# A one-core transformer block: a planner that counts SyncE's issues and the queues' transfers, and a re-cut order of its steps

## The chip, the cores and the metric

The kernel runs on one core of one Trainium2 chip. The metric is device time in microseconds (us), the median of several runs; lower is better. Where one profiled execution is read, its own time and its span are given beside the median. Engines are named as in the profile: PE (TensorE matmul), PEld (its weight loads), DVE (VectorE), ACT (ScalarE), POOL (GpSimd), SP (SyncE, which issues nearly all DMAs from one in-order queue).

## The reference

One transformer block with conditioning, in float32. Eight sequences of 1024 tokens, width 512, 16 heads, hidden width 2048:

```python
mod = silu(condition) @ Wada + bada
sh_a, sc_a, gt_a, sh_m, sc_m, gt_m = split(mod, 6, axis=1)
xm = layernorm(x, g1, be1) * (1 + sc_a) + sh_a
x = x + gt_a * attention(xm, Wqkv, Wproj, bproj)      # causal, softmax
xm = layernorm(x, g2, be2) * (1 + sc_m) + sh_m
x = x + gt_m * (gelu(xm @ W1 + b1) @ W2 + b2)
```

## The kernel before, in words

**Blocks and steps.** The tokens are cut into 16 blocks of 512 (`NB` is 16): block n is the first half (n even) or the second half (n odd) of a sequence; the keys of a second half are twice as many, so odd blocks have more attention. For each block there are dense steps, which the code calls linear: `at` (make the normalized, modulated, transposed input of attention), `k`, `q`, `v`, `proj`, `mt` (the same input for the feed-forward part), `u` 0 to 3 (up) and `d` 0 to 3 (down). `k`, `q`, `v` and `u` are done by seven products of half-size blocks instead of eight (`strassen`), with sums of the weights made once and kept in device memory. All matmuls of one product go through one of three PSUM banks (`lin_bank`).

**Attention.** A group is one block and four heads. Scores units (`scores`, tiles `sc`) only find row maxima, on DVE; weights units (`weights_T`, tiles `st`) compute the scores again, transposed, with the maximum subtracted, and ACT takes the exponential into `pT`. Both use the one PSUM tile `st`, so each unit waits until DVE or ACT has read the one before. POOL masks the diagonal of `pT` (`affine_select`) and adds the units of a group up; `weigh` multiplies by v (tile `po`); `finish` sums over keys, and DVE inverts.

**Who decides the order.** The order of all engines' instructions is decided while the program is built. `plan[w]` lists the dense steps beside the attention of block w; window 16 (`plan[NB]`) holds the rest. A small planner keeps a clock per engine (`now`), notes each instruction with a fixed cost (`note`, `note_pe`, `note_act`), and remembers when each value is written (`written`) and each buffer is left (`left`). Dense steps are generators which yield what they need; `step_aside` and `work` put dense matmuls between attention units until the next unit's needs are met by the planner's clock. `run_jobs`, `run_act_jobs` and `run_pool_jobs` let small DVE, ACT and POOL jobs into those engines' queues when the planner believes them free.

**DMAs before.** Weights come through a ring of eight 256 KB buffers (`RING`, `fetch`, `release`); a weight's load stands in SP's queue as soon as the buffer eight places back is used up, and waits there. The planner of the kernel before has no clock for SP or for the DMA queues: a weight counts as there at once, and other transfers get fixed times: `LANDING` 10000 ns for gate rows, residual tiles and moved k and v, `HOLDING` 8000 ns for each half of a turn. A turn (`turn`) transposes 12 to 14 of the blocks' inputs through device memory: DVE transposes small blocks, one DMA writes them out (`held`), four DMAs read them back in another order (`hat`), ACT or DVE scale them into `xm`.

**Other names the change touches.** `combine_out` (line 193) adds a PSUM bank to something in SBUF on DVE. `either` (lines 158 and 161) puts an addition on DVE or POOL, by the planner's clocks. `bias_row` (line 522) loads one gate row into the single buffer `rowgb`, which the row before it must have left; `project_out` issues it for the feed-forward part at its end, `load_xr` for attention. `scores_by_heads` (lines 1518 to 1535) does a scores unit in two of the banks, when the planner sees no dense work for 3000 ns. `beside` in the plan starts a step as a thread beside the main one.

Of the kernel before, what the change touches and what calls it, by code (L numbers as in the profile page):

```python
# [22 lines left out]
def kernel(  # L23
# [70 lines left out]
    now = {"PE": 0.0, "DVE": 0.0, "ACT": 0.0, "POOL": 0.0}  # L94
# [5 lines left out]
    COLUMN = 0.84  # L100
    table = [None]
# [10 lines left out]
    def note(engine, ns, reads=(), writes=(), port=False):  # L112
        start = max(now[engine], due(reads, writes))
        if port:
            start = max([start] + [b for a, b in pool_spans if a <= start < b])
        end = start + ns
        now[engine] = end
        if engine == "POOL":
            pool_spans.append((start, end))
            del pool_spans[:-16]  # L120
        for k in reads:
            left[k] = max(left.get(k, 0.0), end + SYNC)
        for k in writes:
            written[k] = end + SYNC
        return end

# [112 lines left out]
    for w in range(1, NB):  # L239
# [7 lines left out]
        if w == NB - 1:  # L247
            steps = late[:1] + rows_a + [("proj", n), ("mt", n)] + late[1:]
            steps += rows_m + own + m[3:5] + [("load_xr", w)] + m[5:6]
            late = m[6:]  # L250
        else:
# [9 lines left out]
            steps += [("q", w + 1)] + early_v + rows_m + own  # L261
# [10 lines left out]
    plan[NB] = [late[0], ("beside", late[1]), ("proj", n), ("mt", n)] + mlp_steps(n)  # L272
# [56 lines left out]
    ring, used, taken = [], set(), [0]  # L329

    def fetch():

        while len(ring) < len(order) and (len(ring) < RING or len(ring) - RING in used):
# [24 lines left out]
    def release(*indices):  # L358
        used.update(indices)
        fetch()  # L360
# [23 lines left out]
    def load_x(n):  # L384
# [3 lines left out]
        for t in range(NTT):  # L388
            some = x[b, h * TB + t * P : h * TB + (t + 1) * P, :]
            if f"a{n}" in by_pe:  # L390
                nc.sync.dma_start(rows[:, t, :], some)
            else:
                nc.sync.dma_start(rows[ts(t, Q), :, :], some.rearrange("(t i) d -> i t d", i=Q))
        return rows
# [39 lines left out]
    def modulation(i):  # L434
# [5 lines left out]
        yield [], [BANK]  # L440
        bank = lin_bank()
        pm = banks[bank][:, : NC * B].rearrange("p (c b) -> p c b", b=B)
        for c in range(NC):
            for k in range(NC):
                w = part[k // 2, c // 2][:, k % 2, ts(c % 2, P)]
                matmul(pm[:, c, :], w, condT[:, k, :], k == 0, k == NC - 1, bank=bank)
# [32 lines left out]
    def gates(kind):  # L479
# [11 lines left out]
        yield [], [BANK]  # L491
# [14 lines left out]
        note("DVE", 700, port=True)  # L506
        for name, row in ((f"g{kind}", b_gate), (f"gb{kind}", b_out)):
            kept_rows[name] = kept.tile([B, D], F32, tag=f"kept_{name}", name=f"kept_{name}")
            nc.sync.dma_start(kept_rows[name], row)

    def gate_broadcasts(b, kind):
# [4 lines left out]
        gate_rows[name] = row  # L516

    def bias_row(n, kind):
# [5 lines left out]
        written["row", f"gb{kind}", n] = now["PE"] + LANDING  # L524
# [143 lines left out]
    def turn(key, rows, xm):  # L668
# [17 lines left out]
        written["held", key] = now["PE"] + HOLDING  # L686
# [4 lines left out]
        written["turned", key] = now["PE"] + HOLDING  # L691
# [76 lines left out]
    def accumulate(pairs, reads=(), close=True):  # L768
        yield reads, [BANK]
        bank = lin_bank()  # L770
        for i, (lhsT, rhs) in enumerate(pairs):
            if i:
                yield [], []
            matmul(banks[bank], lhsT, rhs, i == 0, close and i == len(pairs) - 1, reads, bank)
# [11 lines left out]
    def keep(w, i, a, piece):  # L786
        at = kept.tile([P, D], F32, tag=f"kept_{LABEL[id(w)]}_{i}_{a}", name=f"kept_{LABEL[id(w)]}_{i}_{a}")
        kept_sums[id(w), i, a] = at
        nc.sync.dma_start(at, piece)

    def weight_sums(step, part):
# [4 lines left out]
        for j, (out, a, b, op) in enumerate(SUMS):  # L796
# [4 lines left out]
            keep(w, i, out, stage[:, j, :])  # L801
# [5 lines left out]
    def preparation():  # L807
# [5 lines left out]
        def load(w, i):  # L813
# [6 lines left out]
            loaded.append((w, i, got, now["PE"] + 12000))  # L820

        load(*todo.pop(0))
        while loaded:
# [5 lines left out]
            for out, a, b, op, name in IN_PLACE:  # L829
# [3 lines left out]
                keep(w, i, name, got[out])  # L833
# [26 lines left out]
    def strassen(step, x, dest, target, row, done):  # L860
# [14 lines left out]
        def product(a, t, bank=None):  # L875
            start = bank is None
            reads = [(x, t)] + ([("sums", *step, a)] if raw and a[0] == "S" else [])
            for i in range(2):
# [141 lines left out]
    def project_out(n):  # L1020
# [14 lines left out]
        for t, xt in enumerate(tiles):  # L1035
            if last:
# [8 lines left out]
            else:  # L1045
                bank = yield from accumulate(
                    [(attT[:, c, ts(t, P)], piece(at[c])) for c in range(NC)], [("att", n)]
# [18 lines left out]
        bias_row(n, "m")  # L1066
# [3 lines left out]
    def up(step):  # L1070
# [16 lines left out]
        if (n, q) == (0, 0):  # L1087
            yield ["prepared up"], []
        written["g", n, q] = NEVER
# [30 lines left out]
    def store(n, t):  # L1120
        unstored.setdefault(n, 2)

        def when_added():
            yield [("xr", n, 2 * t), ("xr", n, 2 * t + 1)], []
            nc.sync.dma_start(some_rows(out, n, t), residual[n][:, half(t, 2), :])
            unstored[n] -= 1
# [5 lines left out]
    def load_xr(n):  # L1132
# [7 lines left out]
        for t in range(NTT):  # L1140
            written["xr", n, t] = now["PE"] + LANDING
# [3 lines left out]
        row = ("row", "gba", n)  # L1145
        for t in range(NTT):
            job = lambda t=t: add_to(xr[:, t, :], gate_rows["gba"], [row], [("xr", n, t)])
            pool_jobs.append((job, [("xr", n, t), row]))
        written["xr begun", n] = 0.0

    def down(n, part):
# [19 lines left out]
        def product(operand):  # L1171
# [3 lines left out]
            for i in range(NQ):  # L1175
                p = next(at)
                for k in range(2):
# [4 lines left out]
                    for m in range(2):  # L1182
                        if bank is None:
                            yield reads, [BANK]
                            bank = lin_bank()
                        else:
# [5 lines left out]
                            c + m == 0, c == 2 * NQ - 1, reads, bank,  # L1192
# [44 lines left out]
        if part == 0:  # L1237
            yield [("g", n, 0), ("g", n, 1), "prepared", ("row", "gbm", n)], []
            for i in range(NTT):
                add_to(residual[n][:, i, :], gate_rows["gbm"], [("row", "gbm", n)], [("xr", n, i)])  # L1240
            combine(nc.vector, "B12", "B12", "B11")
# [26 lines left out]
        else:  # L1268
# [16 lines left out]
            for q in range(NQ):  # L1285
                hTs.pop((n, q))


    def perform(step):
# [9 lines left out]
        elif kind == "load_xa":  # L1299
            x_pre[step[1]] = load_x(step[1])  # L1300
            written["x", f"a{step[1]}"] = now["PE"] + 6000
# [564 lines left out]
    for n in range(NB):  # L1866
        written["attended", n] = NEVER
        written["v done", n] = NEVER
        written["stored", n] = NEVER
        written["xr begun", n] = NEVER  # L1870
# [75 lines left out]
```

## Time and profile before

| | |
|---|---|
| time, median of 3 runs | 3536.86 us (3535.36 to 3538.43) |
| the profiled execution's own time | 3537.37 us |
| its span, first to last instruction | 3534.7 us |
| mean granted TensorE clock | 0.995 |
| PE busy | 3461.9 us, 98% |
| DVE, POOL, ACT busy | 2201.4, 2054.0, 1208.4 us |

How to read it. Each timeline row is: start in us from the span's start, length in us, engine, line of the kernel, operation, tile written and tiles read, shapes, number of instructions merged into the row, and in brackets the idle time of the engine just before the row with what ended it. Busy PE time includes time at a lowered clock; the rows of stretches give the granted clock (1.00 is full speed) after the busy times of the engines.

### The profile page before, as it was taken

How to read it: one execution, taken by the hardware profiler on the slowest of the kernel's cores; microseconds unless marked ns; L12 is line 12 of the kernel's file. 1: busy time of each engine (PE TensorE's matmuls, PEld its weight loads, DVE VectorE, ACT ScalarE, POOL GpSimd, SP SyncE). 2: the span in 40 equal slices, each digit the busy share in tenths (PEclk: the TensorE clock that was granted, in tenths of full speed). 3: DMA queues.
4: the chain of work that ended last, by engine and by line, in shares of the span. 5: the costliest groups of instructions: out<-in, count | busy, mean ns of one | idle time of the engine just before them, and what ended most of it. 6: DMA issues, size and time to landing. Idle time of an engine off the chain costs nothing. (4 is left out here: it accounts for less than half of the span.)

```text
span 3534.7 us, 120362 instructions
## 1 busy us (share of the span) xinstructions
PE 3461.9 (98%) x54429; PEld 1732.1 (49%) x54429; DVE 2201.4 (62%) x2438; ACT 1208.4 (34%) x1264; POOL 2054.0 (58%) x2228
## 2 busy tenths in 40 slices
PE   8999999999999999999999999999999999999999
PEld 4444445454454545445454444544555445554445
DVE  5776675565657666665566666665666756655463
ACT  2334323352233523335233442333423343223431
POOL 2666846566357663756727566375753658537560
PEclk9999999999999999999999999999999999999999
DMA  6753434435445445353453534545354545443334
GB/s 199 239 167 106 136 115 138 138 112 157 136 127 152 111 155 153 120 160 118 135 155 119 167 112 147 149 138 145 116 158 136 154 130 147 132 134 98 114 91 140
DMA packets 328195, 491.11 MB, mean 139 GB/s; under 512 B 27260, under 2 KB 177596, under 8 KB 324100
## 3 DMA queue, kind: packets, MB, share of 16 engines
q1 hardware_dynamic: 327568, 483.39, 46.1%
q8 instruction: 428, 7.01, 0.8%
q14 instruction: 83, 0.68, 0.1%
q10 hardware_dynamic: 116, 0.03, 0.0%
HBM read 425.57 MB, written 55.64 MB: 136 GB/s over the span
## 5 line engine op out<-in xcount | busy, mean ns | idle before, releaser
L1769 POOL TENSOR_TENSOR pT<-pT,pT 128x256 f32<-128x256 f32 (+3 forms) x1254 | 1214.4, 1003 | 330.0 <-PE po L1679 186.9
L1651 ACT ACTIVATE pT<-st 128x2048 f32<-128x2048 f32 x288 | 541.0, 1878 | 1059.3 <-PE st L1639 952.3
L202 PE MATMUL bank<-w,hT 128*32 128x256 f32 x14336 | 822.7, 380 | 0.5 <-issue 0.5
L1563 DVE TENSOR_REDUCE mx<-sc 128x4 f32<-128x2048 f32 (+3 forms) x381 | 658.9, 1750 | 228.1 <-PE sc L1548 222.3
L202 PEld LDWEIGHTS bank<-w,hT 128*32 128x32 f32 x14336 | 446.5, 110 | 392.7 <-issue 111.6
L202 PE MATMUL bank<-xm_m,w 128*32 128x256 f32 x8192 | 498.5, 382 | 1.6 <-ACT xm_m L750 0.8
L202 PE MATMUL bank<-t_m,w 128*32 128x256 f32 x6144 | 381.6, 380 | 0.6 <-DVE t_m L762 0.6
L1656 POOL TENSOR_SCALAR_AFFINE_SELECT pT<-pT 128x512 f32<-128x512 f32 x256 | 173.6, 696 | 342.3 <-ACT pT L1651 339.8
L202 PEld LDWEIGHTS bank<-xm_m,w 128*32 128x32 f32 x8192 | 256.2, 110 | 223.9 <-issue 56.4
L1560 DVE TENSOR_TENSOR sc<-sc,mask 128x1024 f32<-128x1024 f32 (+1 forms) x158 | 161.5, 1022 | 309.8 <-PE sc L1548 246.5
L1548 PE MATMUL sc<-kT,qT 32*128 32x512 f32 (+3 forms) x3048 | 329.4, 522 | 8.3 <-ACT pT L1651 4.4
L1679 PE MATMUL po<-pT,v 128*32 128x512 f32 (+3 forms) x3048 | 302.0, 491 | 3.8 <-POOL pT L1656 3.6
L1639 PE MATMUL st<-qT,kT 32*128 32x512 f32 (+3 forms) x3072 | 303.8, 488 | 0.0
L202 PEld LDWEIGHTS bank<-t_m,w 128*32 128x32 f32 x6144 | 189.4, 110 | 172.8 <-issue 46.9
L1718 DVE RECIPROCAL rec<-rec 128x128 f32<-128x128 f32 x256 | 227.3, 922 | 49.0 <-ACT rec L1709 49.0
L202 PE MATMUL bank<-xm_a,w 128*32 128x256 f32 x3968 | 241.7, 380 | 0.0
L202 PE MATMUL bank<-w,qT 128*32 128x512 f32 x2048 | 238.4, 599 | 1.1 <-DMA w<-in_L_cond_Wproj_dram 1.1
L1548 PEld LDWEIGHTS sc<-kT,qT 32*128 32x128 f32 x3048 | 130.3, 184 | 191.0 <-issue 94.4
L193 DVE TENSOR_TENSOR hT<-bank,u_u 128x512 f32<-128x512 f32 x192 | 130.4, 687 | 112.0 <-PE bank L202 108.8
L202 PE MATMUL bank<-t_a,w 128*32 128x256 f32 x2944 | 185.3, 381 | 1.4 <-DVE u_d L193 1.4
L1076 ACT ACTIVATE hT<-hT,cols 128x512 f32<-128x512 f32 x256 | 164.6, 711 | 47.8 <-DVE hT L193 47.2
L202 PEld LDWEIGHTS bank<-xm_a,w 128*32 128x32 f32 x3968 | 124.6, 110 | 106.4 <-issue 27.6
(227 smaller groups left out, 3386.3 us busy)
## 6 DMA issues: line engine op xcount, KB each, us to landing
w<-in_L_cond_W_dram SPq DMA_DIRECT2D x384, 256.0 KB
w<-kept_up_S SPq DMA_DIRECT2D x256, 256.0 KB
w<-kept_down_S SPq DMA_DIRECT2D x256, 256.0 KB
w<-kept_qkv_S SPq DMA_DIRECT2D x180, 256.0 KB
w<-in_L_cond_Wqkv_dram SPq DMA_DIRECT2D x147, 256.0 KB
hat_a<-in_x_dram SPq DMA_DIRECT2D x64, 256.0 KB
xr<-in_x_dram SPq DMA_DIRECT2D x32, 512.0 KB
w<-in_L_cond_Wproj_dram SPq DMA_DIRECT2D x64, 256.0 KB
```

Source lines behind the costliest of these rows:

```text
L193: nc.vector.tensor_tensor(out, src, other, op)
L202: nc.tensor.matmul(ps[r, :], columns, rhs, start=start, stop=stop, skip_group_check=True)
L1076: nc.scalar.activation(hT[:, i, :], hT[:, i, :], AF.Gelu, bias=cols[:, O_B1 + f : O_B1 + f + 1])
L1548: nc.tensor.matmul(sc[:, j, c0 : c0 + w], qTs[n][r, gg, ts(qt, P)], keys_of(n, kh)[r, gg, :w], start=True, stop=True, skip_group_check=True,)
L1560: nc.vector.tensor_tensor(place, place, shape_of.to_broadcast(place.shape), ALU.add)
L1563: nc.vector.tensor_reduce(maxima[n, gg][:, kh, qt, :], sc[:, :, c0 : c0 + w], axis=AX.X, op=ALU.max)
L1639: nc.tensor.matmul(st[:, j, c0 : c0 + w], kT[r, gg, ts(k % NTT, P)], qT[r, gg, TB - w :], start=False, stop=True, skip_group_check=True,)
L1651: nc.scalar.activation(pT[:, :, :used], st[:, :, :used], AF.Exp, scale=scale)
L1656: nc.gpsimd.affine_select(diagonal, diagonal, pattern=[[0, HPG], [1, P]], compare_op=ALU.is_ge, fill=0.0, base=0, channel_multiplier=-1,)
L1679: nc.tensor.matmul(po[r, TB - w :], v[:, k % NTT, g * P + j * hd : g * P + (j + 1) * hd], pT[:, j, c0 : c0 + w], start=(k == 0), stop=last ...
L1718: nc.vector.reciprocal(some, some)
L1769: nc.gpsimd.tensor_tensor(into, into, pT[:, j, c0 : c0 + w], ALU.add)
```

## The change

The planner gets clocks for SP and for the DMA queues. `note_dma` adds 425 ns of issue to SP's clock, then lets the transfer begin 1000 ns later or when the queues' clock is free, adds a given length (680 ns for a 256 KB weight, 2600 for `held`, 1250 for each of the four reads back), and takes the data as there 1200 ns after that. It is called at each DMA in place of the fixed times for those (moved k and v keep theirs). Steps now yield the weights that they read, so that the planner lets PE come to a weight only when it believes it landed.

Five things that are not bookkeeping: `combine_out` may copy the bank with ACT and add afterwards, where DVE's clock is 3500 ns behind ACT's; `run_act_jobs` lets jobs into ACT's queue up to 1500 ns ahead of PE's clock; `project_out` starts one waiting POOL job ahead of each tile, and no longer issues the feed-forward gate row at once, but in a thread that waits until the planner believes the row buffer free; the first `u` of the last block waits for the end of `d` of the block before; and the plan is re-cut: `v` stands ahead of `q` in even windows from 4 on, in window 15 `d` 13/2 comes ahead of `proj` 14, and `d` 14/1 moves from window 15 to window 16.

```diff
+    ISSUE, BEGIN, LAND = 425, 1000, 1200
+    def note_dma(ns, reads=(), writes=(), after=0.0):
+        begun = max(now["SP"], due(reads, ()), after)
+        now["SP"] = begun + ISSUE
+        now["DMA"] = max(begun + BEGIN, now["DMA"]) + ns
+        for k in writes:
+            written[k] = now["DMA"] + LAND
...
     def combine_out(out, bank, src, other, reads=(), writes=(), op=ALU.add, last=True):
-        nc.vector.tensor_tensor(out, src, other, op)
-        note("DVE", 690, [("l", bank), *reads], writes)
+        ready = due([("l", bank)], writes)
+        if op is ALU.add and out is not other and max(now["DVE"], ready) > max(now["ACT"], ready) + 3500:
+            nc.scalar.copy(out, src)
+            note_act(585, None, [("l", bank)], writes)
+            either(out, out, other, op, [*reads, *writes], writes)
+        else:
+            nc.vector.tensor_tensor(out, src, other, op)
+            note("DVE", 690, [("l", bank), *reads], writes)
...
         if w == NB - 1:
-            steps = late[:1] + rows_a + [("proj", n), ("mt", n)] + late[1:]
-            steps += rows_m + own + m[3:5] + [("load_xr", w)] + m[5:6]
-            late = m[6:]
+            steps = late[:2] + rows_a + [("proj", n), ("mt", n)] + late[2:]
+            steps += rows_m + own + m[3:5] + [("load_xr", w)]
+            late = m[5:]
...
-            steps += [("q", w + 1)] + early_v + rows_m + own
+            steps += early_v + [("q", w + 1)] + rows_m + own
...
-    plan[NB] = [late[0], ("beside", late[1]), ("proj", n), ("mt", n)] + mlp_steps(n)
+    plan[NB] = late[:-1] + [("beside", late[-1]), ("proj", n), ("mt", n)] + mlp_steps(n)
...
             w = wp.tile([P, D], F32, tag="w", name=f"w_{i}")
+            note_dma(680, [], [("w", i)], freed.get(i - RING, 0.0) + 300)
...
-        yield [], [BANK]
+        yield [("w", i) for i in at], [BANK]
...
-            everything or (min(now["ACT"], now["DVE"]) <= now["PE"] and due(act_jobs[0][1]) <= now["PE"])
+            everything or (min(now["ACT"], now["DVE"]) <= now["PE"] + 1500 and due(act_jobs[0][1]) <= now["PE"])
...
         nc.sync.dma_start(held, small_blocks)
-        written["held", key] = now["PE"] + HOLDING
+        note_dma(2600, [("blocks", key)], [("held", key)])
         yield [("held", key)], []
         for m in range(NTT):
             some = held[:, ts(m, D)].rearrange("(a i) d -> i a d", i=Q)
             nc.sync.dma_start(rows[ts(m, Q), :, :], some)
-        written["turned", key] = now["PE"] + HOLDING
+            note_dma(1250, [("held", key)], [("turned", key)])
...
+            if pool_jobs and not last:
+                pool_jobs.pop(0)[0]()
...
-        bias_row(n, "m")
+        def next_row():
+            yield ["rowgb free"], []
+            bias_row(n, "m")
+        written["row", "gbm", n] = NEVER
+        start(next_row())
...
+        if (n, q) == (NB - 1, 0):
+            yield [("down done", n - 1)], []
```

More of the change, by code (lines that the diff above doesn't have):

```diff
@@ L91 @@
     NB = len(blocks)
-    now = {"PE": 0.0, "DVE": 0.0, "ACT": 0.0, "POOL": 0.0}
+    now = {"PE": 0.0, "DVE": 0.0, "ACT": 0.0, "POOL": 0.0, "SP": 0.0, "DMA": 0.0}
     written, left = {}, {}
@@ L359, in release @@
         used.update(indices)
+        for i in indices:
+            freed.setdefault(i, now["PE"])
         fetch()
@@ L509, in gates @@
             nc.sync.dma_start(kept_rows[name], row)
+            note_dma(200, [("gate", kind)])
     def gate_broadcasts(b, kind):
@@ L523, in bias_row @@
         gate_rows[f"gb{kind}"] = row
-        written["row", f"gb{kind}", n] = now["PE"] + LANDING
+        note_dma(900, ["rowgb free"], [("row", f"gb{kind}", n)])
     jobs = []
@@ L773, in accumulate @@
                 yield [], []
-            matmul(banks[bank], lhsT, rhs, i == 0, close and i == len(pairs) - 1, reads, bank)
+            landed = [("w", i) for i in uses[i : i + 1]]
+            matmul(banks[bank], lhsT, rhs, i == 0, close and i == len(pairs) - 1, [*reads, *landed], bank)
+            if free:
+                freed[uses[i]] = now["PE"]
         return bank
```

48 lines of the change are left out of this document (31 added, 17 removed).

## The prediction

> **What bounds the kernel now.** I read the page's span and shares first, then the timeline of PE for every wait of it, then the stretches with a lowered clock, and then, at the longest waits, the rows of the other engines.
>
> ```profile
> span 3534.7 us, 120362 instructions
> PE 3461.9 (98%) x54429; PEld 1732.1 (49%) x54429; DVE 2201.4 (62%) x2438; ACT 1208.4 (34%) x1264; POOL 2054.0 (58%) x2228
> 0.00:100.00 100.00, 83.54 (x1491) 49.23 (x1491) 61.67 (x91) 28.23 (x34) 37.67 (x56) 1.00 0.63 197
> ```
>
> PE bounds it: 3461.9 of 3534.7 us, so only 72.8 us are idle, 16.5 of them in the first 100 us. The two built orders hold the same matmuls, shape by shape. The change can therefore move only PE's waits, what the clock loses behind them, and PE's changes between kinds of matmul. The waits that I expect it to touch, A to F:
>
> ```profile
> 3404.83 1.07 PE L1679 MATMUL po<-pT,v 128*32 128x384 f32 x16 [1.77 <-POOL pT L1656]
> 3408.41 2.39 PE L1700 MATMUL bank<-pT,ones 128*32 128x512 f32 x8 [2.50 <-POOL pT L1769]
> ...
> 938.75 1.22 PE L1548 MATMUL sc<-kT,qT 32*128 32x512 f32 x8 [2.42 <-DVE mx L1563]
> 943.29 1.22 PE L1518 MATMUL bank<-kT,qT 32*128 32x512 f32 x1 [1.63 <-DVE mx L1535]
> ...
> 1523.52 2.09 PE L1548 MATMUL sc<-kT,qT 32*128 32x512 f32 x8 [3.75 <-ACT pT L1651]
> ...
> 113.73 0.40 PE L202 MATMUL bank<-condT,w 128*32 128x8 f32 x16 [3.05 <-DMA w<-in_L_cond_Wada_dram]
> 114.43 0.83 PE L202 MATMUL bank<-condT,w 128*32 128x8 f32 x48 [0.30 <-DMA w<-in_L_cond_Wada_dram]
> ...
> 3187.93 0.40 PE L1627 MATMUL st<-mrow,minus_ones 32*128 32x512 bf16 x4 [1.08 <-ACT pT L1651]
> 3192.01 0.69 PE L1518 MATMUL bank<-kT,qT 32*128 32x512 f32 x1 [0.77 <-DVE mx L1535]
> 3197.37 0.69 PE L1518 MATMUL bank<-kT,qT 32*128 32x512 f32 x1 [1.10 <-DVE mx L1535]
> ...
> 66.50 0.41 PE L1601 MATMUL bank<-ident_b,mcols 128*32 128x128 bf16 x16 [1.61 <-POOL mcols L1585]
> 152.16 0.60 PE L498 MATMUL bank<-w,condT 128*8 128x256 f32 x2 [1.85 <-DMA w<-in_L_cond_Wada_dram]
> ```
>
> Here the bracket is what counts. A (3404, 3408) is 4.27 us, B (938, 943) 4.05, C (1523) 3.75, D (113) 3.35, E (3187 to 3197) 2.95, F (66, 152) 3.46: 21.8 us. The longest cost more than they last; in these stretches (length, then busy PE, PEld, DVE, ACT, POOL, then the granted clock) the clock is lowered right behind them:
>
> ```profile
> 114.00:121.00 7.00, 6.70 (x128) 3.64 (x124) 1.86 (x3) 2.35 (x2) 1.30 (x3) 0.54 0.97 332
> 223.00:227.00 4.00, 4.00 (x25) 0.75 (x22) 3.55 (x3) 2.13 (x2) 3.92 (x5) 0.59 0.02 4
> 940.00:951.00 11.00, 9.37 (x72) 4.46 (x73) 10.38 (x14) 3.46 (x5) 1.77 (x1) 0.55 0.14 29
> 1524.00:1528.00 4.00, 4.00 (x44) 1.35 (x44) 2.32 (x2) 2.29 (x4) 4.00 (x6) 0.65 0.18 14
> 3408.00:3415.00 7.00, 6.59 (x34) 2.93 (x38) 6.79 (x11) 2.36 (x3) 0.82 (x2) 0.55 0.17 63
> ```
>
> Busy PE time times the missing share of the clock is what each loses: 6.70 x 0.46 = 3.1 (D), 9.37 x 0.45 = 4.2 (B), 4.00 x 0.35 = 1.4 (C), 6.59 x 0.45 = 3.0 (A): 11.7 us. The one at 223 stays (below).
>
> **The change part by part.** To see what the new order does at each place, I counted how much PE work stands between the producer's last input and the consumer in each built order, the cover, at the price of these rows:
>
> ```profile
> 53.64 1.48 PE L202 MATMUL bank<-sums_v,t_a 128*32 128x256 f32 x24
> 55.05 1.15 PE L1548 MATMUL sc<-kT,qT 32*128 32x384 f32 x16
> ...
> 58.31 1.91 PE L202 MATMUL bank<-sums_v,xm_a 128*32 128x256 f32 x32
> 60.04 1.48 PE L202 MATMUL bank<-sums_v,t_a 128*32 128x256 f32 x24
> ```
>
> From start to start 32 matmuls take 1.73 us, so 54 ns each; the 24 ahead of the scores take 1.41, where 1.30 is their share, so a change of kind costs 0.11 us.
>
> A, the re-cut end. Before, only 2.3 us stand between the last weights unit and its `weigh`, and nothing between that and `finish`. With `d` 14/1 moved into window 16 there are 7.4 us ahead of that `weigh`, 3.0 between it and `finish`, and 8.6 behind. The first wait needed 2.3 + 1.77 = 4.1, the second 2.5. Both go, with the clock: -7.3. The shuffle is free, since window 15 still has dense work between its units; if that ran out, E's kind of wait would come back there.
>
> B, `v` ahead of `q`. Before, `v` 5 ran out and four scores units of block 5 stood back to back, one of them by heads. Now `q` 5 comes last, so these units come later and have 2.4 to 3.6 us of `u` 3 between them. The unit by heads, here and in E, is gone from the whole program. -8.3 with the clock. E: between the first weights units of block 15 stood 1.1 to 1.9 us; now it is 1.9 once and 2.8 to 4.4 else, by `d` 13/2 and `proj` 14: -2.9.
>
> C, the gate row. Its rows show a chain over three queues:
>
> ```profile
> 1508.89 0.34 SPq L522 DMA_DIRECT2D row_gbm<-kept_gbm  x1
> 1509.33 1.80 SPq L690 DMA_DIRECT2D hat_a<-held_a  x4
> ...
> 1518.78 2.93 ACT L750 ACTIVATE xm_a<-hat_a,shifta,gaina 128x512 f32<-128x512 f32 x4 [12.43 <-DMA hat_a<-held_a]
> 1521.61 1.85 ACT L1651 ACTIVATE pT<-st 128x2048 f32<-128x2048 f32 x1
> ```
>
> SP stood at the gate row until its buffer was free; `hat_a` stood behind it; ACT waited 12.43 us for `hat_a` with the exponential queued behind; PE waited for that. In the new order `hat_a` of block 8 comes straight behind its `held`, ahead of the row and of the weights. -5.2 with the clock. What the row then meets: only `d` part 0, much later.
>
> D and F, the weights counted. Cover of the third `mod` 3 weight, from the use of its ring buffer: 6.3 us before, 10.0 now, and 6.3 + 3.05 = 9.4 was needed; -6.5 with the clock. The last `gates` weight: 1.7 before, 4.9 now, 3.6 needed. Maxima of block 0's first group: 2.3 before, 4.8 now, 3.9 needed. -3.5.
>
> Sum of gains: 7.3 + 8.3 + 2.9 + 5.2 + 6.5 + 3.5 = 33.7 us.
>
> Against it. Changes of kind go from 1574 to 1584: +1.1. These rows are near new tight places:
>
> ```profile
> 632.10 1.92 PE L202 MATMUL bank<-w,qT 128*32 128x512 f32 x16 [0.23 <-DMA w<-in_L_cond_Wproj_dram]
> ...
> 703.43 0.64 PE L202 MATMUL bank<-xm_m,w 128*32 128x256 f32 x8 [0.80 <-ACT xm_m L750]
> ...
> 929.67 0.38 SPq L685 DMA_DIRECT2D held_m<-xm_m  x1
> 935.15 1.76 SPq L690 DMA_DIRECT2D hat_m<-held_m  x4
> 943.22 2.93 ACT L750 ACTIVATE xm_m<-hat_m,shiftm,gainm 128x512 f32<-128x512 f32 x4 [6.74 <-DMA hat_m<-held_m]
> ```
>
> The third weight of `proj` 2 (632) has 5.2 us of cover where it had 6.9 and already waited 0.23: +1.7. From the end of `proj` 2 to `u` 2 (703, waited 0.80) there are 43.9 us where there were 45.8: +1.9. For block 5 it is 45.1 for 51.9, for block 3 49.6 for 57.9; the shortest turned one is block 13 with 42.9 in both, and PE has no wait for it before; I put 2 us for both, between nothing and 8. The split `combine_out` is used 20 times, off PE's path: at two more instructions of 0.6 to 1.3 us it fits ACT (34% busy) and POOL (58%); were the bank awaited each time, 20 x 0.6 = 12. ACT's jobs let in 1.5 us early do not bunch: 32 stretches between exponentials held four or more scaling jobs, now 28. Sum against: 6.7. The other small waits I take as redrawn at the same sum; 72.8 - 21.8 - 16.5 less the two waits named below leaves some 30 us of them, and a quarter of that, 8 us, could come or go. In their favour speaks the tile `st`, whose readers are these:
>
> ```profile
> L1563 DVE TENSOR_REDUCE mx<-sc 128x4 f32<-128x2048 f32 x189 | 432.8, 2290 | 224.7 <-PE sc L1548 222.3
> L1651 ACT ACTIVATE pT<-st 128x2048 f32<-128x2048 f32 x288 | 541.0, 1878 | 1059.3 <-PE st L1639 952.3 <-POOL pT L1769 81.4 <-POOL mcols L1585 13.7
> ```
>
> Where the work between two units is less than 2.29 or 1.88 us (less for narrower units, 1.0 more with a mask, and 0.25 that I put for handing over), the second must wait. These shortfalls add up to 16.2 us in the order before and to 9.5 in the new one.
>
> Not touched: the first 100 us but for F, and these, whose surroundings are the same in both orders:
>
> ```profile
> 3432.00:3436.00 4.00, 4.00 (x45) 2.15 (x48) 2.08 (x3) 1.84 (x4) 1.41 (x1) 0.65 0.01 4
> ...
> 222.62 0.41 PE L1627 MATMUL st<-mrow,minus_ones 32*128 32x512 bf16 x4 [2.41 <-DVE mx L1563]
> 3429.91 0.33 PE L740 MATMUL bank<-ident,hat_m 128*128 128x128 f32 x1 [2.63 <-ACT hat_m L663]
> ```
>
> Net: 33.7 - 6.7 = 27.0 us. The profiled execution took 3537.4 in all, 2.7 more than its span and 0.5 over the median: 3536.9 - 27.0 = 3509.9, say 3510.
>
> **The rivals.** The clock stays low. Waits of 2.41 us (222.62) and 2.42 (938.75) were followed by 0.59 and 0.55, so I count the clock's 11.7 us as going with the waits. If only a wait as long as C's lowered it, 10.3 of them would not be due to A, B and D, and the time would be 3520. [...] The rows at 223 and 940 speak against that. Chance 0.05.
>
> Some covers don't hold. The plan's own gains (A, B, E: 18.5) stand; C, D and F, which hang on when DMAs land beside others, halve (-7.6), and the small waits grow by 4: 3522. For: at 114 to 121 the DMA share is 0.97. Chance 0.15.
>
> The waits only move. Each piece put elsewhere is missing elsewhere, and the total is what it was: 3530 to 3544. Against: the covers above rise at nearly every kind of wait. Chance 0.10.
>
> Slower: turns reckoned too short. Before, a turn counted 2 x 8.0 = 16.0 us from `held` to data; now 425 + 1000 + 2600 + 1200 and then 425 + 1000 + 4 x 1250 + 1200, 12.85 us. The rows above give 943.22 - 929.67 = 13.55. Where PE comes to `k` or `u` by the planner's clock, it is 0.7 us early; that alone is 26 turns x 0.7 = 18 us at most. It decides once a turn is some 2.4 us late, since then the clock falls as well: 2.5 + 1.4 (C's price) at 9 of the 26 is 35 us, more than the 27: 3545. For: the early `u` of blocks 2, 3 and 5. Against: block 13's 42.9 us without a wait. Chance 0.12.
>
> **How the numbers follow.** All gains with the prices above: 0.58, at 3510; with the first two rivals, 0.78 for faster by over 0.2% (7 us, about what a measurement of this kernel can tell). Within 0.2%: 0.10. Slower: 0.12. Low end: no price but the changes of kind and the small waits 6 us better, 3536.9 - 33.7 + 1.1 - 6 = 3498. High end: into the waits that only move, 3534; beyond it lie the rest of these and the slower case.
>
> **What would show it.** Right: no PE wait over 2 us between 230 and the last block's `hat_m`; the clock lowered twice behind the start (near 223 and at the last `hat_m`) in place of six times; no rows of L1518's kind; PE idle near 57 us; `hat_a` ahead of the gate row. Wrong: PE waits for `xm_m` or `xm_a` behind `hat` DMAs, new stretches at 0.55, or waits at 113 and 1523 that stay.

## The result, and the profile after

| | before | after |
|---|---|---|
| median of 6 runs each | 3537.6 us (3535.4 to 3539.6) | 3506.6 us (3504.3 to 3514.2) |
| ratio, 95% interval | | 0.9917 (0.9904 to 0.9929) |
| the profiled execution's own time | 3537.37 us | 3510.74 us |
| span | 3534.7 us | 3509.0 us |
| PE idle in the span | 72.8 us | 54.8 us |
| PE busy at half clock (granted 0.50), by the trace's records of the granted clock | 31.1 us | 10.9 us |

The change made the kernel 31.0 us faster by the medians; 27.0 was forecast. The two profiled executions differ by 26.6 us, their spans by 25.7. These 25.7 us can be split: PE waits 18.0 us less, half of the 20.2 us less of busy time at half clock is 10.1, and PE's work, reckoned at full clock, takes 2.4 us more. The page of the changed kernel begins so, and the third line is its first 100 us (busy PE, PEld, DVE, ACT, POOL, granted clock):

```profile
span 3509.0 us, 120365 instructions
PE 3454.3 (98%) x54429; PEld 1724.0 (49%) x54429; DVE 2198.9 (63%) x2401; ACT 1212.4 (35%) x1276; POOL 2084.2 (59%) x2258
0.00:100.00 100.00, 85.51 (x1497) 49.16 (x1501) 61.49 (x90) 28.05 (x34) 38.60 (x57) 1.00 0.68 211
```

The matmuls are the same in number (x54429), as they had to be. PE's timeline of the changed kernel has these waits of 1.7 us and more behind the first 140 us (line numbers have moved: L1674 is the old L1627, L1726 the old L1679, L217 the old L202, L764 the old L740):

```profile
150.47 1.03 PE L520 MATMUL bank<-w,condT 128*8 128x256 f32 x4 [1.95 <-DMA w<-in_L_cond_Wada_dram]
...
218.81 0.62 PE L1674 MATMUL st<-mrow,minus_ones 32*128 32x512 bf16 x4 [2.41 <-DVE mx L1610]
...
400.28 0.39 PE L1674 MATMUL st<-mrow,minus_ones 32*128 32x512 bf16 x4 [2.42 <-DVE mx L1610]
...
927.71 2.21 PE L217 MATMUL bank<-xm_m,w 128*32 128x256 f32 x32 [2.04 <-ACT xm_m L774]
...
3368.08 1.06 PE L1726 MATMUL po<-pT,v 128*32 128x512 f32 x8 [1.70 <-POOL pT L1703]
...
3403.57 0.47 PE L764 MATMUL bank<-ident,hat_m 128*128 128x128 f32 x1 [2.69 <-ACT hat_m L687]
```

Gone are 113 (3.05 us), 938 and 943 (2.42, 1.63), 1523 (3.75), 66 (1.61), the three at 3187 to 3197, and the wait of 2.50 at the last `finish`. The stretches around the longest waits, and that of the old wait at 114 for comparison:

```profile
114.00:121.00 7.00, 6.22 (x124) 2.99 (x120) 4.12 (x6) 2.94 (x3) 4.68 (x7) 1.00 1.05 379
217.00:226.00 9.00, 7.19 (x39) 2.67 (x39) 6.78 (x6) 3.07 (x3) 8.77 (x10) 0.62 0.01 3
398.00:406.00 8.00, 5.70 (x91) 2.55 (x95) 4.19 (x5) 3.83 (x4) 7.00 (x10) 1.00 0.32 107
924.00:935.00 11.00, 8.27 (x132) 3.78 (x128) 4.14 (x7) 3.51 (x5) 1.79 (x1) 1.00 0.59 179
3402.00:3412.00 10.00, 8.20 (x86) 5.35 (x90) 3.64 (x10) 4.62 (x7) 3.07 (x3) 0.66 0.17 54
```

Up to PE's last matmul the clock is now lowered twice, from 217.6 and from 3402.2, 6.8 us each; before, it was lowered six times, 34.1 us in all. Both stretches begin 1.2 to 1.3 us before the wait there is over, so part of each falls on idle time (PE is busy for 5.6 and 5.3 us of the 6.8). The waits at 400 and at 927 cost no clock.

### The profile page after: what moved, and what is told of

Its sections match the earlier page's. It is cut to its first block, busy times and chain, and to the rows that moved or that the text cites. A ratio compares the mean times of both kernels' runs of the same rounds, so it can differ in the third digit from the quotient of the medians.

```text
span 3509.0 us, 120365 instructions
## 1 busy us (share of the span) xinstructions
PE 3454.3 (98%) x54429; PEld 1724.0 (49%) x54429; DVE 2198.9 (63%) x2401; ACT 1212.4 (35%) x1276; POOL 2084.2 (59%) x2258
## 4 chain that ended last, share of the span: by engine, by line
PE 83%; POOL 7%; DMA 3%; DVE 3%; ACT 1%; issue 1%; SPq 1%; ACTq 0%; DVEq 0%; POOLq 0%
PE bank L217 59%; PE sc L1595 8%; PE st L1686 6%; PE po L1726 6%; POOL pT L1816 4%; PE st L1674 2%; PE bank L1747 2%; DMA hat_m<-held_m 1%; DVE mx L1610 1%; POOL hT L170 1%; ACT pT L1698 1%; DMA held_m<-xm_m 1%; PE bank L1648 0%; POOL xr L170 0%; DMA w<-in_L_cond_Wqkv_dram 0%
## 5 line engine op out<-in xcount | busy, mean ns | idle before, releaser
L217 PE MATMUL bank<-w,hT 128*32 128x256 f32 x14336 | 823.7, 380 | 0.4 <-issue 0.4
L217 PEld LDWEIGHTS bank<-w,hT 128*32 128x32 f32 x14336 | 446.7, 110 | 390.3 <-issue 105.8
L217 PE MATMUL bank<-xm_m,w 128*32 128x256 f32 x8192 | 498.6, 381 | 3.6 <-ACT xm_m L774 2.2
L217 PE MATMUL bank<-t_m,w 128*32 128x256 f32 x6144 | 382.4, 380 | 0.9 <-DVE t_m L786 0.6
L217 PEld LDWEIGHTS bank<-xm_m,w 128*32 128x32 f32 x8192 | 255.6, 110 | 231.2 <-issue 62.2
L1726 PE MATMUL po<-pT,v 128*32 128x512 f32 (+3 forms) x3048 | 301.6, 490 | 3.9 <-POOL pT L1703 3.9
L217 PEld LDWEIGHTS bank<-t_m,w 128*32 128x32 f32 x6144 | 189.6, 110 | 172.9 <-issue 48.5
L217 PE MATMUL bank<-xm_a,w 128*32 128x256 f32 x3968 | 243.4, 382 | 0.4 <-DMA w<-in_L_cond_Wqkv_dram 0.4
L217 PE MATMUL bank<-w,qT 128*32 128x512 f32 x2048 | 237.0, 595 | 1.1 <-DMA w<-in_L_cond_Wproj_dram 0.7
L217 PE MATMUL bank<-t_a,w 128*32 128x256 f32 x2944 | 183.2, 380 | 0.0
L217 PEld LDWEIGHTS bank<-xm_a,w 128*32 128x32 f32 x3968 | 123.5, 110 | 110.3 <-issue 29.3
```

What stands on the lines that cost most here:

```text
L217: nc.tensor.matmul(ps[r, :], columns, rhs, start=start, stop=stop, skip_group_check=True)
L1726: nc.tensor.matmul(po[r, TB - w :], v[:, k % NTT, g * P + j * hd : g * P + (j + 1) * hd], pT[:, j, c0 : c0 + w], start=(k == 0), stop=last ...
```

## The experiments

Every kernel was run 4 to 9 times beside the kernel before. The ratio's interval is in the table; 0.001 is 3.5 us. "Idle" and "half clock" (PE busy at half clock) are those of the profiled execution, as above. Two of these stand high among the executions of their kernel: 3534.91 us in `no_small` and 3510.04 in `no_pool_early`, 7.1 and 6.5 over the median. Rows whose intervals overlap are not told apart by these runs.

| run | what it is | median, us | ratio (95%) | idle | half clock |
|---|---|---|---|---|---|
| plan_only | before, with the re-cut plan alone | 3528.2 | 0.9972 (0.9962 to 0.9982) | 67.7 | 24.0 |
| no_plan | after, with the plan of before | 3517.7 | 0.9947 (0.9934 to 0.9961) | 61.5 | 9.3 |
| weights_at_once | after, weights not accounted | 3515.3 | 0.9937 (0.9925 to 0.9949) | 60.2 | 9.9 |
| turn_16 | after, a turn counted 3.2 us longer | 3515.2 | 0.9937 (0.9925 to 0.9950) | 55.9 | 9.2 |
| land_1800 | after, all data taken as there 0.6 us later | 3512.9 | 0.9930 (0.9917 to 0.9943) | 55.3 | 11.2 |
| row_at_once | after, gate row issued at once | 3510.1 | 0.9918 (0.9904 to 0.9931) | 55.3 | 10.2 |
| row_and_turn | both of these undone | 3517.1 | 0.9944 (0.9932 to 0.9956) | 53.6 | 19.1 |
| no_split | after, without the split `combine_out` | 3510.2 | 0.9920 (0.9906 to 0.9935) | 56.4 | 13.2 |
| no_act_early | after, without ACT's 1500 ns | 3508.3 | 0.9916 (0.9901 to 0.9931) | 53.1 | 11.9 |
| no_pool_early | after, without POOL's job ahead of a `proj` tile | 3503.5 | 0.9898 (0.9882 to 0.9915) | 53.1 | 16.1 |
| no_split_no_act | after, without split and 1500 ns | 3526.8 | 0.9962 (0.9948 to 0.9976) | 68.2 | 23.5 |
| no_small | after, without any of the three | 3527.9 | 0.9972 (0.9962 to 0.9981) | 73.2 | 25.1 |

**The plan, alone and taken out.** `plan_only` makes to the kernel before the diff's changes of `plan` and the wait of the last block's first `u`; two of its places:

```diff
-            steps = late[:1] + rows_a + [("proj", n), ("mt", n)] + late[1:]
+            steps = late[:2] + rows_a + [("proj", n), ("mt", n)] + late[2:]
...
-            steps += [("q", w + 1)] + early_v + rows_m + own
+            steps += early_v + [("q", w + 1)] + rows_m + own
```

> The kernel before with nothing of the change but the re-cut plan (v ahead of q, d 13/2 ahead of proj 14, d 14/1 in window 16, and the guard on the last u that this needs). Theory: the parts of the prediction add up, and the plan carries A, B and E, 18.5 us of 33.7; the built order keeps one unit by heads and the cover of 6.3 and 1.7 us for the mod 3 and gates weights, so D, C and F stay: about 3519 us, the waits at 3404 and 3408 gone, those near 113, 152 and 1523 there. Rival: the planner's DMA accounts do it and the plan alone moves waits about: 3530 us or more.

It was 9.9 us faster than before by the ratio (6 to 13), not 18.5. PE's timeline, and one stretch of its clock, say which part failed:

```profile
114.62 0.40 PE L202 MATMUL bank<-condT,w 128*32 128x8 f32 x16 [3.70 <-DMA w<-in_L_cond_Wada_dram]
...
935.28 0.69 PE L1521 MATMUL bank<-kT,qT 32*128 32x512 f32 x1 [2.15 <-DVE mx L1538]
...
1522.38 1.48 PE L1551 MATMUL sc<-kT,qT 32*128 32x512 f32 x8 [3.37 <-ACT pT L1654]
...
3382.20 1.06 PE L1682 MATMUL po<-pT,v 128*32 128x512 f32 x8 [1.69 <-POOL pT L1659]
...
934.00:945.00 11.00, 9.72 (x73) 3.44 (x77) 6.71 (x12) 3.66 (x4) 1.44 (x2) 0.69 0.41 85
```

C and D stand, as they should. E is gone. Of A, one wait of 1.69 us is left. B is not gone: in this order block 5 still has a unit by heads, with a wait of 2.15 us and 6.8 us at half clock (0.69 over these 11 us). The plan alone does not keep block 5's units apart.

`no_plan` is the other half of the pair: the changed kernel with the old lines of `plan`.

> The changed kernel with the plan of before. Theory: A (7.3 us) and E (2.9 us) come back, since the built order has 2.3 and 0.9 us of cover at the end again; of B only a shortfall of 1.2 us comes back, since no two units of block 5 stand without work between them: about 3518 us. Rival that the plan is all of it: 3537 us. Rival that the plan is nothing: 3507 us.

Here the forecast held, 3517.7 us. Its timeline has A and E again, and of B one wait:

```profile
957.39 1.15 PE L1595 MATMUL sc<-kT,qT 32*128 32x256 f32 x16 [1.54 <-DVE mx L1610]
...
3174.95 0.69 PE L1565 MATMUL bank<-kT,qT 32*128 32x512 f32 x1 [0.77 <-DVE mx L1582]
...
3387.42 1.07 PE L1726 MATMUL po<-pT,v 128*32 128x384 f32 x16 [1.77 <-POOL pT L1703]
3391.00 2.38 PE L1747 MATMUL bank<-pT,ones 128*32 128x512 f32 x8 [2.50 <-POOL pT L1816]
```

So the plan was worth about 10 us from either side, 9.9 in the kernel before and 10.6 in the kernel after (0.9947 against 0.9917). B is mostly not the plan's: with the old plan and the rest of the change one wait of 1.54 us is left of it, no unit by heads stands there (the only two are at 3173 to 3181) and the clock is not lowered: the 16 matmuls at 957.39 take 1.15 us, as 16 of that shape do in the changed kernel at 966.22.

**The weights.** `weights_at_once` counts a ring weight as there at once again, and drops the accounts of the prepared sums; the rest of the change stays.

```diff
-            note_dma(680, [], [("w", i)], freed.get(i - RING, 0.0) + 300)
+            note_dma(680, [], [], freed.get(i - RING, 0.0) + 300)
```

> The changed kernel, with ring weights counted as there at once, as before, and without the accounts of the prepared weight sums' loads and stores; plan, row and turn stay. In the built order the covers of the mod 3 weights (6.3 and 10.0 us) and of the last gates weight (1.7 us) are exactly those of the kernel before. Theory: D and F's gates wait come back, 3.35 + 1.85 us and 3.1 of clock, at places near 113 and 150, and nothing else: 3514 us. Rival: they were chance and the time stays at 3507.

```profile
113.56 0.31 PE L217 MATMUL bank<-condT,w 128*32 128x8 f32 x16 [2.07 <-DMA w<-in_L_cond_Wada_dram]
...
151.22 0.60 PE L520 MATMUL bank<-w,condT 128*8 128x256 f32 x2 [2.80 <-DMA w<-in_L_cond_Wada_dram]
```

A wait at D's place is back, with 3.4 us at half clock behind it (the 16 matmuls of `st` at 115.04 take 1.79 us, the same at 351.45 take 1.09), though 2.07 us long where it was 3.05. The wait for the last `gates` weight, which the changed kernel has too (1.95 us), is longer. F's other wait, for `mcols`, is back at 67.31 with its 1.61 us. The time is 3515.3 where 3514 was expected. That D goes with the weights' accounts is shown: it is here and in `plan_only`, and not in the runs that keep these accounts.

**How long a turn is reckoned.** `turn_16` was meant to give the turn its old 16.0 us within the new accounts. The sums of 12.85 us in the prediction and of 16.0 here count 425 ns of issue in each half. In the code these 425 ns move SP's clock alone; the transfer begins 1000 ns after the start of the issue. With the queues' clock free a turn is therefore reckoned at 1000 + 2600 + 1200 and 1000 + 4 x 1250 + 1200, 12.0 us, and in `turn_16` at 15.2.

```diff
-        note_dma(2600, [("blocks", key)], [("held", key)])
+        note_dma(5375, [("blocks", key)], [("held", key)])
...
-            note_dma(1250, [("held", key)], [("turned", key)])
+            note_dma(1344, [("held", key)], [("turned", key)])
```

> The changed kernel, with the two halves of a turn reckoned at 16.0 us together as before (held 5375, each read back 1344 ns). Theory: the shorter reckoning (12.85 us) is part of the gain, because u and k come earlier: with 16.0 the shortfalls at the st tile grow from 9.5 to 14.6 us in the built order, one unit by heads comes back, and hat_a of block 8 stands behind four weights again: 3512 to 3517 us. Rival (the prediction's slower case): the reckoning is too short and costs waits for xm such as the 2.04 us at u of block 3; with 16.0 the time falls to 3504 us or less.

The longer reckoning costs 7 us (3515.2; the two intervals overlap by a hair), so the shorter one is no loss as a whole. It may be one at block 3's third `u`. In the changed kernel `held_m` was issued at 909.74, and PE waited 2.04 us for `xm_m`, which ACT began 17.11 us later, at 926.85, where the planner reckons 12.0. With the longer reckoning the wait is 1.38 us; but it also varies with the short one, from 1.84 us in `row_at_once` to none in `no_split`:

```profile
913.72 0.49 SPq L709 DMA_DIRECT2D held_m<-xm_m  x1
...
931.16 1.34 PE L217 MATMUL bank<-xm_m,w 128*32 128x256 f32 x16 [1.38 <-ACT xm_m L774]
```

`land_1800` takes every transfer's data as there 0.6 us later; it was meant to cover that place and the `gates` weight. (By the code a weight then counts as there 3.5 us after its issue begins, and a turn takes 13.2; the expectation below adds the 425 ns again.)

```diff
-    ISSUE, BEGIN, LAND = 425, 1000, 1200
+    ISSUE, BEGIN, LAND = 425, 1000, 1800
```

> The changed kernel with LAND 1800 for 1200 ns, so that a weight counts as there 3.9 us after its issue begins and a turn takes 14.05 us; the traces show 4.5 us for the last gates weight (147.66 to 152.16) and 13.55 for a turn. Built order: cover of the last gates weight 11.1 us for 4.9, no zero cover between sc 1/1 and st 1/0 (the wait of 2.41 near 218), shortfall at st 7.7 us for 9.5. Theory: these two waits and the clock behind them go, 2.0 + 2.4 + 1.7 to 3.4: 3501 us. Rival: waiting longer for data only moves the waits: 3507 us or more.

The rival was right: 3512.9 us. In its timeline the `gates` weight's wait and those at 218 and 400 are gone, and block 3's is 0.85 us. But PE waits 2.08 us at 151, and a weight of `proj` that was in time in the changed kernel comes late, with a granted clock of 0.60 around it:

```profile
179.82 1.93 PE L217 MATMUL bank<-w,qT 128*32 128x512 f32 x8 [5.59 <-DMA w<-in_L_cond_Wproj_dram]
...
176.00:184.00 8.00, 4.18 (x28) 1.62 (x32) 2.32 (x2) 0.00 (x0) 5.28 (x5) 0.60 0.99 313
```

**The gate row.** In the changed kernel SP issues `hat_a` of block 8 ahead of the row, and ACT does not wait for `hat_a`:

```profile
1485.33 0.32 SPq L709 DMA_DIRECT2D held_a<-xm_a  x1
...
1489.51 1.74 SPq L714 DMA_DIRECT2D hat_a<-held_a  x4
...
1494.71 0.42 SPq L546 DMA_DIRECT2D row_gbm<-kept_gbm  x1
...
1497.60 2.93 ACT L774 ACTIVATE xm_a<-hat_a,shifta,gaina 128x512 f32<-128x512 f32 x4
```

`row_at_once` takes the row's thread away, and the planner's account no longer lets SP wait for the row's buffer.

```diff
-        def next_row():
-            yield ["rowgb free"], []
-            bias_row(n, "m")
-        written["row", "gbm", n] = NEVER
-        start(next_row())
+        bias_row(n, "m")
...
-        note_dma(900, ["rowgb free"], [("row", f"gb{kind}", n)])
+        note_dma(900, [], [("row", f"gb{kind}", n)])
```

> The changed kernel, with the feed-forward gate row issued at once at the end of proj again. Theory as the prediction had it for C: SP stands at the row, hat_a behind it, ACT behind that, and PE's wait of 3.75 us near 1523 comes back with its lowered clock: 3512 us. Rival: in the built order hat_a of block 8 still comes straight behind its held and ahead of the row, so that the shorter reckoning of the turn, not the row's thread, took C away: 3507 us, no wait there, though SP stands some 30 us at L546 in all.

No wait came back, and the time stayed (3510.1). So taking away the thread alone does not bring C back; `hat_a` is still ahead of the row (1489.16 and 1493.68). `row_and_turn` therefore undoes the thread and the turn's length together, which puts the row ahead of `hat_a` again.

> The changed kernel with both things undone that bear on C: the gate row issued at once, and the turn reckoned at 16.0 us. Each alone had no wait at 1523; in this built order hat_a of block 8 stands behind four weights and the gate row again, as in the kernel before. Theory (C is SP's queue order, and either half of the change takes it away): the wait of 3 to 4 us of PE behind ACT near 1515 comes back, with its lowered clock: 3520 us, 5 more than turn_16 (3515.2). Rival (C was the sum of queues on that day's order and not the row): no wait there and 3515 us.

```profile
1498.92 0.42 SPq L546 DMA_DIRECT2D row_gbm<-kept_gbm  x1
1499.44 1.80 SPq L714 DMA_DIRECT2D hat_a<-held_a  x4
...
1510.03 2.93 ACT L774 ACTIVATE xm_a<-hat_a,shifta,gaina 128x512 f32<-128x512 f32 x4 [8.03 <-DMA hat_a<-held_a]
...
1513.77 1.86 ACT L1693 ACTIVATE pT<-st 128x2048 f32<-128x2048 f32 x1
...
1515.68 1.14 PE L1590 MATMUL sc<-kT,qT 32*128 32x512 f32 x8 [0.27 <-ACT pT L1693]
```

The first half of C's chain is back in these rows: the row, `hat_a` behind it, ACT idle for 8.03 us. The second half is not: PE had come to the transposed scores only at 1510.58, when `hat_a` was there, and waited 0.27 us for the exponential. Nor does the row's place make ACT idle. In `turn_16`, where `hat_a` is ahead of the row, ACT waits nearly as long:

```profile
1496.11 1.83 SPq L714 DMA_DIRECT2D hat_a<-held_a  x4
...
1498.04 0.38 SPq L546 DMA_DIRECT2D row_gbm<-kept_gbm  x1
...
1506.25 2.93 ACT L774 ACTIVATE xm_a<-hat_a,shifta,gaina 128x512 f32<-128x512 f32 x4 [7.08 <-DMA hat_a<-held_a]
```

What these two runs share is the longer reckoning, which puts four weights ahead of `hat_a`: it is issued 9.4 and 9.9 us after its `held_a`, against 4.2 us in the changed kernel (14.9 before). So the shorter reckoning is what spares ACT here. In the kernel before, SP also stood at the row: 5.1 us lie between the end of the weights' issue (1503.80) and the row's (1508.89). In `row_and_turn` the row follows the weights at once (1498.83 and 1498.92), so this part of C was not brought back, and what took it away is not shown. Whether the idle ACT costs anything hangs on where PE stands at that time, and which edit moved PE there was not pinned.

**The three small edits.** They had been costed at nothing. `no_small` takes all three out:

```diff
-        if op is ALU.add and out is not other and max(now["DVE"], ready) > max(now["ACT"], ready) + 3500:
+        if False:
...
-            everything or (min(now["ACT"], now["DVE"]) <= now["PE"] + 1500 and due(act_jobs[0][1]) <= now["PE"])
+            everything or (min(now["ACT"], now["DVE"]) <= now["PE"] and due(act_jobs[0][1]) <= now["PE"])
...
-            if pool_jobs and not last:
-                pool_jobs.pop(0)[0]()
```

> The changed kernel without three edits together: combine_out never split to ACT, ACT's jobs not let in ahead of PE's clock, no POOL job started ahead of a tile of proj. Theory of the prediction: they are worth nothing by themselves (the built order's shortfall at st is 9.7 us against 9.5): 3507 us, at most 3 off. Rival: freeing DVE by the split is a part of the gain: 3512 us or more.

It lost 21.3 us of the 31.0: 3527.9. Its longest wait is at block 3's third `u`, the place of the 2.04 us:

```profile
935.79 1.08 PE L217 MATMUL bank<-xm_m,w 128*32 128x256 f32 x8 [6.05 <-ACT xm_m L774]
```

Next, each edit was taken out by itself.

> The changed kernel with combine_out never split to ACT, the other two small edits kept. The three together were worth 21 us, against the prediction's nothing. Theory: the split is most of it: where DVE is 3.5 us behind, 0.6 us of ACT frees a PSUM bank and the turn's transposes are not held up on DVE: 3520 us or more, with PE waits behind ACT or DVE for xm, qT and mcols. Rival (the jobs of ACT let in early, or the POOL job ahead of each tile, carry it): 3507 to 3510 us here.

> The changed kernel with ACT's jobs not let in 1500 ns ahead of PE's clock, the other two small edits kept. Theory (the split carries the 21 us): 3507 us, at most 4 off. Rival: hat tiles come later on ACT and with them the turns, so that PE waits for xm at u of block 3 and others: 3515 us or more.

> The changed kernel without the POOL job started ahead of each tile of proj, the other two small edits kept. Theory (the split carries the 21 us): 3507 us, at most 3 off; the residual's first addition only moves on POOL, 59% busy. Rival: without it the additions come all at the end of proj (run_pool_jobs there), statistics and hat_m are late, and PE waits for xm_m: 3515 us or more.

3510.2, 3508.3 and 3503.5 us: no one of them is worth anything that these runs can tell (all three intervals overlap that of the changed kernel, also that of `no_pool_early`, whose median is the lowest). My theory that the split carries the 21 us fell. Last, split and 1500 ns out together, POOL's job left in:

> The changed kernel without the split `combine_out` and without ACT's 1500 ns; the job that POOL starts ahead of each `proj` tile stays. Without all three the kernel took 3527.85 us, 21 more than with them, with a wait of 6.05 us at 935.79, at `u` of block 3 for `xm_m`, and `held_m` of that block issued at 918.82; without any one it took 3503.5 to 3510.2, `held_m` at 907 to 910. Theory: split and ACT's 1500 ns are the pair, either of which keeps DVE's and ACT's queues short enough ahead of block 3's turn, and POOL's job is worth nothing: 3524 to 3531 us, `held_m` near 918 and the wait near 935 of 4 us or more. Rival: POOL's job is a third stand-in, which is enough by itself: 3505 to 3513 us, `held_m` near 909, no wait of 4 us there. Something between, say 3516 to 3521, would say that the 21 us are several small waits, each with its own cause.

3526.8 us: the pair makes the difference, and either of the two is enough while POOL's job is left in. What they do at block 3 can be followed. In the kernel without both:

```profile
898.52 1.53 ACT L660 ACTIVATE hat_m<-xr,offset_m,rstd_m 128x512 f32<-128x512 f32 x2
...
904.27 0.83 ACT L660 ACTIVATE hat_m<-xr,offset_m,rstd_m 128x512 f32<-128x512 f32 x1
...
907.72 0.68 DVE L655 TENSOR_SCALAR hat_m<-xr,rstd_m,offset_m 128x512 f32<-128x512 f32 x1
...
915.33 0.42 SPq L709 DMA_DIRECT2D held_m<-xm_m  x1
...
931.93 1.08 PE L217 MATMUL bank<-xm_m,w 128*32 128x256 f32 x8 [5.69 <-ACT xm_m L774]
...
926.00:938.00 12.00, 6.31 (x72) 2.40 (x72) 6.57 (x5) 3.51 (x5) 1.79 (x1) 0.72 0.42 101
```

and in the changed kernel:

```profile
899.02 2.23 ACT L660 ACTIVATE hat_m<-xr,offset_m,rstd_m 128x512 f32<-128x512 f32 x3
901.54 0.54 DVE L655 TENSOR_SCALAR hat_m<-xr,rstd_m,offset_m 128x512 f32<-128x512 f32 x1
...
902.54 1.88 ACT L1698 ACTIVATE pT<-st 128x2048 f32<-128x2048 f32 x1 [1.29 <-PE st L1686]
...
909.74 0.38 SPq L709 DMA_DIRECT2D held_m<-xm_m  x1
```

Four tiles `hat_m` must be scaled, and then transposed on DVE, before the turn can start. In the changed kernel three of them go into ACT's queue ahead of the exponential at 902.54, and the fourth is done on DVE at 901.54. Without the pair the third stands behind the exponential, at 904.27, the fourth comes on DVE at 907.72, and the transposes follow it, one by one, between additions that wait for PE's banks (1.36, 0.36 and 0.42 us); the last two begin at 913.76. `held_m` is 5.6 us later, and the wait is 5.69 us in place of 2.04. Of the clock's 6.8 us at half speed half falls on the wait itself; the busy 6.31 us of the row above times 0.28 is 1.8 us lost. That makes 3.65 + 1.8 = 5.4 us at this one place.

The exponential alone does not decide it. In `no_act_early`, without the 1500 ns but with the split, a third and a fourth tile stand behind the exponential too (it began at 900.56):

```profile
902.33 0.81 ACT L660 ACTIVATE hat_m<-xr,offset_m,rstd_m 128x512 f32<-128x512 f32 x1
...
903.50 0.82 ACT L660 ACTIVATE hat_m<-xr,offset_m,rstd_m 128x512 f32<-128x512 f32 x1
...
904.91 1.89 DVE L700 STREAM_TRANSPOSE xm_m<-hat_m 128x512 f32<-128x512 f32 x3
...
908.70 0.32 SPq L709 DMA_DIRECT2D held_m<-xm_m  x1
```

But the fourth is on ACT, three transposes come in one go, and PE waits 0.57 us for `xm_m`. So the two edits reach the same by different ways here: the one puts a tile ahead of the exponential, the other keeps the last tile off DVE's queue.

The rest is spread: without the pair the profiled kernel has 13.5 us more idle time and 12.6 us more of busy time at half clock (6.3 us lost), at waits of 1.0 to 3.6 us from 31 to 3014 us, behind different producers. How the split alone makes up for the missing 1500 ns in those places was not traced. Nor was it tested what the small edits do in a kernel without the new accounts.

## Why the prediction was right, and where its steps were not

**The total.** The forecast of PE's idle time (near 57 us) and of the clock (11.7 us gained) came out at 54.8 and 10.1. The work at full clock grew by 2.4 us, where 1.1 was put for changes of kind; the other 1.3 were not pinned. The sum was right, its parts less so.

**A**, 7.3 us. The wait at `finish` is gone, but the first moved to an earlier `weigh` of the same end (3368.08, 1.70 us); nearly every kernel with the re-cut plan has it (1.69 us in `plan_only`). 4.27 - 1.70 and the clock's 3.0 make 5.6. The step that failed is the cover of one named unit taken for the cover of all units of that stretch.

**B**, 8.3 us, and the 2 us put against it. Both as forecast: no unit by heads, no lowered clock, and 2.04 us for `xm_m` at 927. But it was counted among the plan's own gains, and `plan_only` shows that the plan alone leaves 2.15 us and half clock there, while `no_plan`, without the new plan, leaves 1.54 us and no lowered clock. The step that failed is the edit to which the gain was put down: the new accounts and not the order of `v` and `q` carry most of B.

**C**, 5.2 us. Gone, with `hat_a` ahead of the row, as forecast. The chain over three queues stood correctly in the rows of before. But which edit cuts it stays open in part: without the row's thread nothing returned, and with the longer turn ACT waited again (7.08 us) and PE did not.

**D and E**, 6.5 and 2.9 us. Gone. E returned in `no_plan`, and D in `weights_at_once` at 2.07 of its 3.05 us and half of its lowered clock. **F**, 3.5 us: half. The wait for `mcols` is gone, and returned with D; the last `gates` weight waits 1.95 us where it waited 1.85. The step that failed takes the cover that is needed as fixed. It was 1.7 + 1.85 = 3.6 us before, but 4.9 + 1.95 = 6.9 after, and 4.5 in `weights_at_once`, whose order has a cover of 1.7 there and waits 2.80: it is not one number. In the rows, 4.5 us lie between the last such load's issue and PE's use before (147.66 to 152.16), 5.9 in `weights_at_once` (145.29 to 151.22) and 11.0 in the changed kernel (139.46 to 150.47). Whether this hangs on what else the queues carry was not shown; their DMA share at 114 to 121 is 1.05 in the changed kernel.

**Against.** `proj` 2's weight waits 0.73 where it waited 0.23, so +0.5 in place of +1.7; `u` 2 waits nowhere near 703, in place of +1.9.

**Not touched.** The waits at 223 and at the last `hat_m` stayed at 2.41 and about 2.7 us, as forecast, but the clock stayed low for 6.8 us at each, where it was 3.4. PE was busy for 10.9 us of that, in place of 6.8: 2.0 us lost that no step had. And a new wait of 2.42 came at 400.

**The small edits at nothing.** This is the step that failed most. Each alone is worth nothing, as `no_split`, `no_act_early` and `no_pool_early` show; split and 1500 ns together are worth 20 us. I had costed each by the time that its instructions take and by whether they bunch, not by what they do to the chain of jobs ahead of a transfer that feeds PE. The plan was worth 10 us instead of the 18.5 that I gave it; plan and accounts without the small edits stand at 3527.9, where the plan alone stands at 3528.2. That the total was met is partly luck: an overpriced plan and accounts against small edits priced at nothing, and the mechanism of most of their 20 us is not known beyond block 3.

**The rivals.** The clock's loss went with the waits (31.1 us of busy time at half clock before, 10.9 after; rival one falls), and the waits did not only move. "Some covers don't hold" was true at the `gates` weight, and not in the total. The slower case, turns reckoned too short, shows at most at one place (2.04 us); `turn_16` shows that longer turns cost 7 us more than they save. Its working had a slip: with a turn reckoned at 12.0 us and not 12.85, PE is 1.55 us early and not 0.7, and the bound is 26 x 1.55 = 40 us and not 18. The case was nearer than its price said, and still did not come.

## What to carry to other kernels

In an order that a planner builds, price an edit by the chain that it lets pass, not by its instructions: look for the jobs on which the next transfer hangs, and ask what each of them now stands behind on its engine's queue, to the last one. Parts that do the same for the order can stand in for each other, so take them out alone and together before calling one of them worthless. A cover computed for one unit holds for that unit only; list the waits of the whole stretch.

## What was not expected of the hardware

Waits of the same length and kind were followed by a lowered TensorE clock in some places and not in others. In the changed kernel the wait of 2.42 us at 400.28 left it at 1.00 (the row 398 to 406 above). In `row_at_once` the same unit waited as long, and 3.4 us at half clock followed (8.00 x 0.21 / 0.50, from the row of the stretch):

```profile
397.13 0.40 PE L1669 MATMUL st<-mrow,minus_ones 32*128 32x512 bf16 x4 [2.42 <-DVE mx L1605]
...
396.00:404.00 8.00, 6.87 (x84) 2.90 (x88) 3.04 (x4) 3.41 (x4) 6.97 (x10) 0.79 0.30 100
```

In the kernel before and in the changed kernel the granted clock is 0.50 in all eight lowered stretches up to PE's last matmul; three of them last 3.4 us, four 6.8 and one 10.2. Waits of 2.41 and 2.42 us were followed by such a stretch in two places (222.62 in the kernel before, 397.13 in `row_at_once`). For a forecast of this kernel it follows that the clock's price of a wait near 2.4 us is a chance, not a number: at such waits these traces show nothing (400.28 in the changed kernel), 1.7 us (397.13 in `row_at_once`) or 2.8 us lost (218.81 in the changed kernel).
